# Running sums over four key tiles in an attention block, and values issued behind the scores

## The chip, the cores and the metric

The kernel runs on one core of one Trainium2 chip. Its time is the device time in microseconds, as the median of several runs. The engines are named as in the profile: PE (matrix products), PEld (its weight loads), DVE (vector), ACT (activations), POOL (GpSimd), SP (here only an issuer of DMAs). A name with a trailing q is an engine's sequencer, which issues DMAs and waits.

## The reference

One transformer block, on x of 2 x 1024 tokens x 1024 features, all in fp32:

```
h = layernorm(x)
q, k, v = split(h @ qkvw + qkvb)              # 32 heads of 32
x = x + softmax(q k^T / sqrt(32)) v @ ow + ob
h = layernorm(x)
x = x + (silu(h @ W_gate.T) * (h @ W_up.T)) @ W_down.T     # width 2752
```

The change is in the softmax and in the product with the values. For a head and a query, every exponential p[key] is needed twice: in the sum over keys of p[key] v[key], and in the plain sum over keys of p[key], by which the first is divided later.

## The kernel before

**Units and phases.** Attention is cut into 64 units. A unit is two heads (`u`), one half of a batch's queries (512), and all 1024 keys. Sixteen units make a phase: phase 0 is batch 0's first half of queries, phase 3 is batch 1's second half. A unit goes through its keys in NT = 8 tiles of 128 (`kt`). The probabilities of one key tile are a tile `p` of 128 keys x 1024 (512 queries of two heads); there is a ring of RING = 8 + 3 + 4 + 4 = 19 such buffers.

**What happens to a key tile.** `scores` (L500) makes two key tiles at a time: 8 PE instructions into two PSUM tiles `s`, at L509. DVE folds each into a running maximum `top` (`largest`, L525), and ACT copies it out into its `p` (`keep`, L528). When all eight are there, `maximum` (L541) reduces `top` over keys and spreads the negated maximum back over the partitions, through DRAM, as `m`. Then, tile by tile, `less_maximum` (L579) adds `m` (L582, on POOL, in phase 0 on DVE for every fourth tile), and `exponential` (L590) runs on ACT (L591). `values` (L610) multiplies with V: for each key tile four products of 256 columns (two heads, two halves of the queries), which use four column groups of PE at once. That is 8 PE instructions, at L620, into the PSUM tile `acc`.

**How the sums are made.** The plain sum over keys is also a PE product, with a matrix of `ones` in place of V (also at L620: again 8 PE instructions for a tile, called a block of ones here). To need fewer of these, tiles are first added in place: in phases 1 to 3 the odd tile gets the even one added (`add`, L601 to L605), and the ones product is made for odd tiles only (`summed`). In phase 0 the fourth tile of four also gets the second added, and the ones product is made once in four tiles. Since an in-place sum spoils the tile for the values, `differences` (L593, on POOL) rewrites V first: if p1 holds p0 + p1, then p0 (v0 - v1) + (p0 + p1) v1 is what was wanted. The adds run on DVE in phase 0, and on POOL and DVE by turns afterwards.

**Runs.** `values` is issued for RUN = 4 key tiles at a time, so each unit has two runs; in phases 1 to 3 a run is 16 instructions with V, a block of ones, and the same again. At the end of a unit ACT copies `acc` out (`finish`, L636), and SP stores the context and the sums (L644, L646). Once a quarter of a phase is done, POOL multiplies the context by the reciprocal sums (L730), for the output projection (L782).

**The order of the work.** Everything is in an order written out by the program. `attention_steps` (L650) writes a list of steps along score tiles n = 0, 1, 2, ...: each is a *beat*. At beat n it issues the scores (even n), the subtraction of the maximum for the tile NT + LAG = 11 beats back, and then the run of values that ended 14 beats back. `Emitter.run` (L66) interleaves this list with a list of filling work: the projections of q, k and v in phase 0, then the output projection and the feed-forward network of the phase before (its products are at L924 and L1073, and DVE adds the results at L1086). It keeps an estimated clock, on which each PE step costs its `cost` and everything else nothing. `em.later(delay, fn)` has a step issued when that clock is `delay` ns further on, and `needs=` holds a step back until what it names has been issued. None of this waits at run time: it only sets each engine's order of instructions, and each engine works through its own in that order.

Of the kernel before, what the change touches and what calls it, by code (L numbers as in the profile page):

```python
# [12 lines left out]
ALU = mybir.AluOpType  # L13
# [117 lines left out]
def preln_block_kernel(  # L131
# [14 lines left out]
    nc = tc.nc  # L146
# [3 lines left out]
    NT = S // P  # L150
# [9 lines left out]
    MM4, MM1 = 855.0, 230.0  # L160
    UNITS = HEADS // 2
    QTR = 4
    LAG = 3
    RUN = 4
    RING = NT + LAG + RUN + 4

    const = ctx.enter_context(tc.tile_pool(name="const", bufs=1))
    lin = ctx.enter_context(tc.tile_pool(name="lin", bufs=1))
# [25 lines left out]
    def Pt(name):  # L194
        return att.tile([P, S], F32, tag="p", bufs=RING, name=name)

# [32 lines left out]
    em = Emitter()  # L229
# [234 lines left out]
    class Unit:  # L464
# [35 lines left out]
        def scores(self, i):  # L500

            kts = (2 * i, 2 * i + 1)
            ps = [
                psum.tile([P, S], F32, tag="s", bufs=2, name=f"s_{self.name}_{kt}") for kt in kts
            ]
            for a in range(2):
                for h in range(2):
                    rows = slice((2 * a + h) * HD, (2 * a + h + 1) * HD)
                    nc.tensor.matmul(  # L509
                        ps[a][:, h * NH : (h + 1) * NH],  # L510
                        self.k[rows, i * P : (i + 1) * P],
                        self.q[rows, :],
                        start=True,
                        stop=True,
                    )


            for kt in kts:
                self.p[kt] = Pt(f"p_{self.name}_{kt}")

            def largest(kt, s):
                if kt == 1:
                    self.top = att.tile([P, S], F32, tag="top", bufs=1, name=f"top_{self.name}")
                if kt > 0:
                    nc.vector.tensor_tensor(self.top, s, self.p[0] if kt == 1 else self.top, ALU.max)  # L525

            def keep(kt, s):
                nc.scalar.copy(self.p[kt], s)  # L528

            if i == 0:  # L530
                keep(0, ps[0])
                em.later(2600.0, lambda: largest(1, ps[1]))
            else:
                largest(kts[0], ps[0])
                em.later(1600.0, lambda: keep(kts[0], ps[0]))
                em.later(1700.0, lambda: largest(kts[1], ps[1]))
            em.later(3300.0 if i > 0 else 4200.0, lambda: keep(kts[1], ps[1]))
            if kts[1] == NT - 1:
                self.maximum()
# [39 lines left out]
        def less_maximum(self, kt):  # L579
            p = self.p[kt]  # L580
            eng = nc.vector if self.phase == 0 and kt % 4 == 3 else nc.gpsimd
            eng.tensor_tensor(p, p, self.m, ALU.add)  # L582
            em.later(3500.0, lambda: self.exponential(kt))
            if kt % 2 == 1:
                twice = self.phase == 0 and kt % 4 == 3
                em.later(8100.0, lambda: self.add(kt, 1), None if twice else ("added", self.n, kt))
                if twice:
                    em.later(9900.0, lambda: self.add(kt, 2), ("added", self.n, kt))

        def exponential(self, kt):  # L590
            nc.scalar.activation(self.p[kt], self.p[kt], AF.Exp, scale=SCALE)  # L591

        def differences(self):  # L593

            v = self.v.rearrange("p (i a) n -> p i a n", a=2)
            nc.gpsimd.tensor_tensor(v[:, :, 0, :], v[:, :, 0, :], v[:, :, 1, :], ALU.subtract)
            if self.phase == 0:
                v = self.v.rearrange("p (i a) n -> p i a n", a=4)
                nc.gpsimd.tensor_tensor(v[:, :, 1, :], v[:, :, 1, :], v[:, :, 3, :], ALU.subtract)

        def add(self, kt, back):  # L601


            eng = nc.vector if self.phase == 0 or kt % RUN == RUN - 1 else nc.gpsimd
            eng.tensor_tensor(self.p[kt], self.p[kt], self.p[kt - back], ALU.add)  # L605

        def summed(self, kt):
            return kt % (4 if self.phase == 0 else 2) == (3 if self.phase == 0 else 1)

        def values(self, kt):  # L610

# [38 lines left out]
    def attention_steps(cuts):  # L650


        units = [Unit(n) for n in range(B * NS * UNITS)]
        lists = [Steps()]
        total = len(units) * NT
        q = lists[0]

        def load_step(k, i):
            if k < len(units):
                q.add(lambda: units[k].load(i), needs=("qk", units[k].b, units[k].g))  # L660

        for i in range(2):
            load_step(0, i)
        for n in range(total + NT + LAG + 3):
            if n in cuts:
                q = Steps()
                lists.append(q)
            k, kt = divmod(n, NT)
            if n < total:
                if kt == 1 or kt == 3:  # L670
                    load_step(k + 1, kt // 2)
                if n == 0:
                    q.add(lambda: em.later(9000.0, lambda: None, ("first",)))
                    q.add(lambda: None, needs=("first",))
                if kt == NT - 2:
                    q.add(units[k].load_v, needs=("v", units[k].b, units[k].hf))
            if n < total and kt % 2 == 0:
                q.add(lambda k=k, i=kt // 2: units[k].scores(i), MM4, beat=True)
            else:
                q.add(lambda: None, beat=True)  # L680
            k, kt = divmod(n - NT - LAG, NT)
            if 0 <= k < len(units):
                if kt == 0:
                    q.add(units[k].differences)
                q.add(lambda k=k, kt=kt: units[k].less_maximum(kt), needs=("max", k))
            k, kt = divmod(n - NT - LAG - 3, NT)
            if 0 <= k < len(units) and kt % RUN == RUN - 1:
                q.add(lambda: None, needs=("added", k, kt))
                for v in range(kt - RUN + 1, kt + 1):
                    cost = MM4 / 2 * (1 + units[k].summed(v))  # L690
                    q.add(lambda k=k, v=v: units[k].values(v), cost)
        return lists


# [453 lines left out]
    def weight_sum_steps():  # L1148
        q = Steps()

        def start(i):
# [42 lines left out]
            for j, args in enumerate(todo):  # L1194
                em.later(8500.0 + 3000.0 * j, lambda args=args: add(*args))
                em.later(16000.0 + 2500.0 * j, lambda j=j: store(j))
# [13 lines left out]
    with tc.manual_schedule():  # L1210
# [81 lines left out]

        rests = [rest(n) for n in range(B * NS)]
        lists = attention_steps([(n + 1) * UNITS * NT + 2 * NT for n in range(B * NS - 1)])
        side = [*prep_ctx(0), *prep_ctx(1)]
        em.run(head)
# [58 lines left out]
```

## Time and profile before

| | |
|---|---|
| runs before | 3269.68, 3277.49, 3278.75 us; median 3277.49 |
| profiled execution | 3264.24 us; span of its instructions 3262.5 us |
| granted TensorE clock, mean of the span | 0.996 |
| attention, first scores to last values | 90.8 to 2776.7 us |
| DVE adds L605, shortest / median / longest | 1162 / 1226 / 6904 ns |
| POOL adds L605, shortest / median / longest | 2342 / 2359 / 2827 ns |
| POOL busy in 200 us, 200 to 400 (phase 0) | 144.6 us |
| POOL busy in 200 us, 1200 to 1400 (phase 1) | 117.9 us |

In the lines of groups, "x480 | 1193.3, 2508 | 11.5 <-DVE top L525 8.4" reads: 480 instructions, 1193.3 us busy in all, 2508 ns each on average; the engine sat idle for 11.5 us in front of them, 8.4 of it until the DVE instruction at L525 was done. PE's instructions overlap each other, four at a time in the tiled products, so their duration is longer than the time from one start to the next. A fp32 product is two PE instructions. In a line of the timeline the first number is the start in us, the second the length, and a bracket at the end tells the idle time before it and what ended it.

### The profile page before, as it was taken

The numbers are of one execution on the slowest core, as the hardware profiler recorded it, in microseconds if no ns is written. First come the engines' busy times: TensorE is split into PE (matmuls) and PEld (weight loads), VectorE is DVE, ScalarE is ACT, GpSimd is POOL, SyncE is SP. The second block draws the span as 40 slices with busy tenths as digits, with TensorE's granted clock in tenths as the row PEclk, the third lists the DMA queues.
The fourth block names the chain that finished last, engine by engine and source line by source line (L and its number), as shares of the span: only waits on it lengthen the run. The fifth ranks groups of instructions, "written<-read, shape, count | busy, mean of one in ns | idle before, by whom it ended". The sixth has DMA issues, their size and how long they took to land.

```text
span 3262.5 us, 43853 instructions
## 1 busy us (share of the span) xinstructions
PE 3206.8 (98%) x16256; PEld 1792.5 (55%) x16256; DVE 1999.2 (61%) x2733; ACT 1432.7 (44%) x1570; POOL 1767.8 (54%) x871
## 2 busy tenths in 40 slices
PE   8999999999999999999999999999999999999999
PEld 4444444444346565663466555634666567477775
DVE  2266676666356677667766777676677774344334
ACT  2244554444456555554565555545655554010000
POOL 0267766776676555667766665667756555200000
PEclk9999999999999999999999999999999999999999
DMA  4566666655435444446344444463444444544442
GB/s 155 170 183 197 219 197 205 194 173 170 140 107 149 146 147 148 146 149 205 104 142 146 146 143 143 143 201 101 142 147 149 144 139 139 178 156 152 154 153 96
DMA packets 337828, 507.31 MB, mean 155 GB/s; under 512 B 105424, under 2 KB 122064, under 8 KB 337616
## 3 DMA queue, kind: packets, MB, share of 16 engines
q1 hardware_dynamic: 281424, 405.91, 39.9%
q10 hardware_dynamic: 56192, 98.60, 9.8%
q8 instruction: 130, 2.13, 0.3%
q14 instruction: 82, 0.67, 0.1%
HBM read 429.14 MB, written 75.24 MB: 155 GB/s over the span
## 4 chain that ended last, share of the span: by engine, by line
PE 86%; DVE 6%; DMA 3%; POOL 2%; issue 1%; ACT 1%; SPq 0%; ACTq 0%; POOLq 0%; DVEq 0%
PE p L924 31%; PE pq L370 11%; PE pd L1073 11%; PE acc L620 9%; PE s L509 7%; PE pvv L432 7%; PE po L782 7%; DVE top L525 1%; DVE x L1086 1%; POOL p L582 1%; DMA ctx<-dctx 1%; DMA rec<-drec 1%; PE pg L968 1%; PE pd L1000 1%; DVE p L605 1%
## 5 line engine op out<-in xcount | busy, mean ns | idle before, releaser
L582 POOL TENSOR_TENSOR p<-p,m 128x1024 f32<-128x1024 f32 x480 | 1193.3, 2508 | 11.5 <-DVE top L525 8.4
L528 ACT COPY p<-s 128x1024 f32<-128x1024 f32 x512 | 516.7, 1011 | 840.3 <-DVE top L525 642.1
L591 ACT ACTIVATE p<-p 128x1024 f32<-128x1024 f32 x512 | 533.2, 1057 | 270.0 <-POOL p L582 246.2
L525 DVE TENSOR_TENSOR top<-s,top 128x1024 f32<-128x1024 f32 x384 | 468.0, 1219 | 275.1 <-PE s L509 266.1
L924 PE MATMUL p<-sum,m 128*128 128x256 f32 x2688 | 616.7, 383 | 4.1 <-DVE sum L906 3.6
L924 PEld LDWEIGHTS p<-sum,m 128*128 128x128 f32 x2688 | 503.0, 190 | 126.5 <-issue 45.7
L605 POOL TENSOR_TENSOR p<-p,p 128x1024 f32<-128x1024 f32 x96 | 227.1, 2366 | 629.7 <-ACT p L591 595.6
L924 PE MATMUL p<-xn2T,m 128*128 128x256 f32 x2016 | 471.1, 383 | 5.2 <-DVE sum L833 2.4
L370 PE MATMUL pq<-xnT,wqk 128*128 128x512 f32 x1024 | 463.2, 601 | 0.0
L1073 PE MATMUL pd<-wp,h 128*128 128x512 f32 x960 | 438.0, 602 | 10.3 <-DVE x L1086 9.9
L924 PEld LDWEIGHTS p<-xn2T,m 128*128 128x128 f32 x2016 | 376.7, 190 | 104.4 <-issue 47.9
L605 DVE TENSOR_TENSOR p<-p,p 128x1024 f32<-128x1024 f32 x192 | 335.7, 1748 | 135.5 <-ACT p L591 134.8
L370 PEld LDWEIGHTS pq<-xnT,wqk 128*128 128x128 f32 x1024 | 188.2, 190 | 255.9 <-issue 252.7
L1073 PEld LDWEIGHTS pd<-wp,h 128*128 128x128 f32 x960 | 177.1, 190 | 248.1 <-issue 200.0
L509 PE MATMUL s<-q,k 32*128 32x512 f32 x2048 | 302.2, 643 | 10.6 <-ACT p L528 10.5
L1086 DVE TENSOR_TENSOR x<-pd,x 128x512 f32<-128x512 f32 x360 | 236.7, 681 | 71.1 <-PE pd L1073 70.6
L620 PE MATMUL acc<-p,vals 128*32 128x256 f32 x4096 | 266.2, 382 | 5.5 <-DVE p L605 5.4
L1186 POOL TENSOR_TENSOR ws<-raw 128x512 f32<-128x512 f32 x62 | 89.3, 1440 | 300.5 <-DMA raw<-in_w_gu 188.9
L432 PE MATMUL pvv<-wv,xnT 128*128 128x512 f32 x512 | 234.3, 603 | 2.4 <-ACT xnT L266 2.4
L782 PE MATMUL po<-wo,ctx 128*128 128x512 f32 x512 | 234.4, 608 | 0.0
L620 PEld LDWEIGHTS acc<-p,vals 128*32 128x32 f32 x4096 | 119.5, 109 | 147.3 <-issue 71.3
L952 ACT ACTIVATE gate<-gate 128x512 f32<-128x512 f32 x84 | 52.9, 630 | 278.0 <-DVE gate L951 277.4
(94 smaller groups left out, 2476.9 us busy)
## 6 DMA issues: line engine op xcount, KB each, us to landing
m<-dws SPq DMA_DIRECT2D x336, 256.0 KB
m<-in_w_gu SPq DMA_DIRECT2D x252, 256.0 KB
wp<-ddn SPq DMA_DIRECT2D x160, 256.0 KB
m<-d SPq DMA_DIRECT2D x64, 512.0 KB
wp<-in_w_dn SPq DMA_DIRECT2D x120, 256.0 KB
raw<-in_w_gu ACTq DMA_DIRECT2D x84, 256.0 KB
dws<-ws ACTq DMA_DIRECT2D x84, 256.0 KB
x<-in_x SPq DMA_DIRECT2D x32, 512.0 KB
```

Of the source, the lines that this page charges most:

```text
L370: nc.tensor.matmul(ps, wqk[b, g, w, hk][:, k, :], xnT[b, s][:, kc, :], start=(kc == 0), stop=(kc == KC - 1),)
L432: nc.tensor.matmul(st["ps"], xnT[b, t // TB][:, kc, (t % TB) * P : (t % TB + 1) * P], st["w"][kc], start=(kc == 0), stop=(kc == KC - 1),)
L509: nc.tensor.matmul(ps[a][:, h * NH : (h + 1) * NH], self.k[rows, i * P : (i + 1) * P], self.q[rows, :], start=True, stop=True,)
L525: nc.vector.tensor_tensor(self.top, s, self.p[0] if kt == 1 else self.top, ALU.max)
L528: nc.scalar.copy(self.p[kt], s)
L582: eng.tensor_tensor(p, p, self.m, ALU.add)
L591: nc.scalar.activation(self.p[kt], self.p[kt], AF.Exp, scale=SCALE)
L605: eng.tensor_tensor(self.p[kt], self.p[kt], self.p[kt - back], ALU.add)
L620: nc.tensor.matmul(self.acc[j * HD : (j + 1) * HD, c : c + NQ], w(h), self.p[kt][:, q0 : q0 + NQ], start=start, stop=stop, skip_group_chec ...
L782: nc.tensor.matmul(st["ps"], ctxT[b, blk][:, g, t * P : (t + 1) * P], st["w"][hf, g], start=(g == 0), stop=(g == G - 1),)
L924: nc.tensor.matmul(ps, mats[c, n][:, kc, :], rhs, start=(kc == 0), stop=(kc == hk - 1),)
L1073: nc.tensor.matmul(st["pd"], lefts[n](pi)[:, j, t * P : (t + 1) * P], st["wp", pi, n, j], start=(j == 0), stop=(j == PART // 2 - 1),)
```

## The change

There is now one scheme for all phases, SUMS = 4. In every run of four tiles the second gets the first added, the third the second, the fourth the third, so the fourth holds all four; the ones product is made for the fourth only. `differences` has three subtractions, v0 - v1, v1 - v2, v2 - v3, for all tiles of a unit at once. In phase 0 all adds are DVE's, issued 8.1 us behind the subtraction of the maximum; in the others the fourth tile's add is DVE's, 12.5 us behind, and the second and third tile's are POOL's, 11.0 us behind. An add whose predecessor has not been issued yet is put off by 0.5 us.

The run of values is issued one beat later, 15 beats behind its last tile, and directly behind that beat's scores, ahead of the subtraction of the maximum. A `p` buffer is taken when the score copy into it is issued, and no longer with the scores. The values of V are loaded one beat later too.

```diff
+    SUMS = 4
...
-            for kt in kts:
-                self.p[kt] = Pt(f"p_{self.name}_{kt}")
...
             def keep(kt, s):
+
+                self.p[kt] = Pt(f"p_{self.name}_{kt}")
                 nc.scalar.copy(self.p[kt], s)
...
             em.later(3500.0, lambda: self.exponential(kt))
-            if kt % 2 == 1:
-                twice = self.phase == 0 and kt % 4 == 3
-                em.later(8100.0, lambda: self.add(kt, 1), None if twice else ("added", self.n, kt))
-                if twice:
-                    em.later(9900.0, lambda: self.add(kt, 2), ("added", self.n, kt))
+            if kt % SUMS > 0:
+
+                vec = self.phase == 0 or kt % RUN == RUN - 1
+                delay = 8100.0 if self.phase == 0 else 12500.0 if vec else 11000.0
+                eng = nc.vector if vec else nc.gpsimd
+                em.later(delay, lambda: self.add(kt, eng))
...
-            v = self.v.rearrange("p (i a) n -> p i a n", a=2)
-            nc.gpsimd.tensor_tensor(v[:, :, 0, :], v[:, :, 0, :], v[:, :, 1, :], ALU.subtract)
-            if self.phase == 0:
-                v = self.v.rearrange("p (i a) n -> p i a n", a=4)
-                nc.gpsimd.tensor_tensor(v[:, :, 1, :], v[:, :, 1, :], v[:, :, 3, :], ALU.subtract)
-
-        def add(self, kt, back):
-
-
-            eng = nc.vector if self.phase == 0 or kt % RUN == RUN - 1 else nc.gpsimd
-            eng.tensor_tensor(self.p[kt], self.p[kt], self.p[kt - back], ALU.add)
+            v = self.v.rearrange("p (i a) n -> p i a n", a=SUMS)
+            for a in range(SUMS - 1):
+                nc.gpsimd.tensor_tensor(v[:, :, a, :], v[:, :, a, :], v[:, :, a + 1, :], ALU.subtract)
+
+        def add(self, kt, eng):
+
+            if kt % SUMS > 1 and ("added", self.n, kt - 1) not in em.done:
+                em.later(500.0, lambda: self.add(kt, eng))
+                return
+            eng.tensor_tensor(self.p[kt], self.p[kt], self.p[kt - 1], ALU.add)
+            em.done.add(("added", self.n, kt))
 
         def summed(self, kt):
-            return kt % (4 if self.phase == 0 else 2) == (3 if self.phase == 0 else 1)
+            return kt % SUMS == SUMS - 1
...
-        for n in range(total + NT + LAG + 3):
+        for n in range(total + NT + LAG + 4):
...
-                if kt == NT - 2:
+                if kt == NT - 1:
                     q.add(units[k].load_v, needs=("v", units[k].b, units[k].hf))
...
                 q.add(lambda: None, beat=True)
+
+            k, kt = divmod(n - NT - LAG - 4, NT)
+            if 0 <= k < len(units) and kt % RUN == RUN - 1:
+                q.add(lambda: None, needs=("added", k, kt))
+                for v in range(kt - RUN + 1, kt + 1):
+                    cost = MM4 / 2 * (1 + units[k].summed(v))
+                    q.add(lambda k=k, v=v: units[k].values(v), cost)
             k, kt = divmod(n - NT - LAG, NT)
...
-            k, kt = divmod(n - NT - LAG - 3, NT)
-            if 0 <= k < len(units) and kt % RUN == RUN - 1:
-                q.add(lambda: None, needs=("added", k, kt))
-                for v in range(kt - RUN + 1, kt + 1):
-                    cost = MM4 / 2 * (1 + units[k].summed(v))
-                    q.add(lambda k=k, v=v: units[k].values(v), cost)
```

## The prediction

> **What bounds the kernel now.** I read the page first, then the groups of instructions by shape, then the timeline of one stretch in the third phase of attention, then the waits, and last the start of the fourth phase. The page and the groups give the loads:
>
> ```profile
> span 3262.5 us, 43853 instructions
> PE 3206.8 (98%) x16256; PEld 1792.5 (55%) x16256; DVE 1999.2 (61%) x2733; ACT 1432.7 (44%) x1570; POOL 1767.8 (54%) x871
> ```
>
> ```profile
> L582 POOL TENSOR_TENSOR p<-p,m 128x1024 f32<-128x1024 f32 x480 | 1193.3, 2508 | 11.5 <-DVE top L525 8.4 <-DMA m<-d 3.0
> L605 DVE TENSOR_TENSOR p<-p,p 128x1024 f32<-128x1024 f32 x192 | 335.7, 1748 | 135.5 <-ACT p L591 134.8
> L605 POOL TENSOR_TENSOR p<-p,p 128x1024 f32<-128x1024 f32 x96 | 227.1, 2366 | 629.7 <-ACT p L591 595.6 <-DMA q<-dq 15.5 <-DMA m<-dws 9.7
> L620 PE MATMUL acc<-p,ones 128*32 128x256 f32 x1792 | 138.4, 381 | 0.0
> ```
>
> PE is busy 98% of the span; its idle time is 55.7 us in all, so the kernel's time is PE's work, and any PE instruction that goes away shortens it unless another engine then makes PE wait. The other engines have room on average: POOL 54%, DVE 61%. The timeline shows what a PE step really costs (matmuls overlap, so I read starts, not durations):
>
> ```profile
> 1704.72 5.31 PE L1073 MATMUL pd<-wp,h 128*128 128x512 f32 x12
> 1709.96 1.14 PE L509 MATMUL s<-q,k 32*128 32x512 f32 x8
> 1711.04 3.70 PE L1073 MATMUL pd<-wp,h 128*128 128x512 f32 x8
> 1714.67 1.07 PE L620 MATMUL acc<-p,vals 128*32 128x256 f32 x16
> 1715.55 0.61 PE L620 MATMUL acc<-p,ones 128*32 128x256 f32 x8
> 1715.99 1.05 PE L620 MATMUL acc<-p,vals 128*32 128x256 f32 x16
> 1716.85 0.61 PE L620 MATMUL acc<-p,ones 128*32 128x256 f32 x8
> 1717.39 1.98 PE L1073 MATMUL pd<-wp,h 128*128 128x512 f32 x4
> ```
>
> One block of ones (8 instructions) lasts from 1715.55 to 1715.99, 0.44 us. A run of values (four key tiles) stands alone between weight products, 3.6 us after the scores. Pairs of scores follow each other at about 10.2 us (1709.96, then 1720.17), so a score tile, the program's beat, is about 5.1 us.
>
> **The change on PE.** Phase 0 already summed over four tiles. Phases 1 to 3 summed over two, 48 units with four blocks of ones each; now two each. That takes away 48 x 2 = 96 blocks x 0.44 = 42.2 us of PE, with nothing put in its place on PE. (Before there are 1792 / 8 = 224 blocks; after, 128.) All of it lies on the path, since PE has no idle time to hide it in.
>
> Values also move behind scores. Each change between whole-array products and the tiled ones costs something: a 512-column instruction inside a stretch takes 0.43 us, so 12 of them from 1704.72 should end at 1709.88, and the scores start at 1709.96; the ones of 1716.85 should hand over at 1717.29 and do so at 1717.39. That is 0.08 to 0.10, say 0.09 us a change. Before, one run and its neighbouring scores have four such changes (into and out of each); after, three, if scores to values costs like the others. No scores stand directly before values in the trace, so the price of that change is open: free would save two changes, 0.18 x 128 runs = 23 us; twice as dear would save none, 0 us. The Trainium skill, TensorEngine Tiling (Array Packing), Key Properties, says that a change of tiling mode drains the engine, and scores (32 rows) and values (32 columns) are different modes, so I take the middle: 0.09 x 128 = 11.5 us. PE in sum: -53.7 us.
>
> **The sums on POOL and DVE.** The sum of a run is now a chain: tile 1 adds tile 0, tile 2 adds that, tile 3 adds that. In phases 1 to 3 tiles 1 and 2 are added on POOL, tile 3 on DVE; before, one add of each run was POOL's and one DVE's. So DVE keeps its 192 adds, POOL gets 96 more x 2.37 = 227 us. The differences of the values grow from one or two to three a unit. The small form (128x128) averages 630 ns against 880 for the old 128x256 one: 48 x (1.89 - 0.88) + 16 x 0.38 = 55 us. POOL goes from 1768 to about 2050 us. Per run of phases 1 to 3, about 20.4 us long, this is 2.9 us more. What covers it is POOL's own waiting (in the waits: total us, times, longest):
>
> ```profile
> POOL p L605 <- ACT p L591: 595.6, 80, 13.8
> ...
> DVE p L605 <- ACT p L591: 134.8, 48, 9.3
> ```
>
> and PE's own waits, which are few (total us, times, longest):
>
> ```profile
> PE s L509 <- ACT p L528: 10.5, 5, 3.9
> ...
> PE acc L620 <- DVE p L605: 5.4, 3, 2.1
> ```
>
> POOL runs ahead of the rest and then stands 7.4 us on average (595.6 / 80) before its one add of a run until ACT has made the exponential. An idle 7.4 us takes 2.9 more us of work without anybody noticing. The adds are also issued later: 11.0 us behind the subtraction on POOL and 12.5 us on DVE instead of 8.1, with the exponential still at 3.5, so POOL finds its operand ready more often. I cost the steady stretches at nothing on PE; if that cover were gone, ACT would wait for the late subtraction L582 in front of an exponential, its score copies behind it would be late, and PE would wait at L509.
>
> DVE now waits for POOL's second add. Behind that add in DVE's queue stand the evictions of the weight products (L1086 and its like) and the maxima, and PE waits for both. The POOL add of tile 2 is issued 12.5 + 5.1 - 11.0 = 6.6 us ahead of the DVE add and lasts 2.4, so POOL must be over 4.2 us behind before it hurts.
>
> A rule speaks against moving sums to POOL. The row: the DVE add with both inputs in SBUF averages 1748 ns, while the maximum of the same size that reads PSUM averages 1219. The Trainium skill, SBUF — State Buffer, Who interferes with whom, says that such a two-input DVE instruction and a POOL instruction reading SBUF exclude each other for the whole instruction. By the rule, POOL's share in phases 1 to 3 (1308 of 2042 us busy, by the view of stretches) rises by 275 / 2042 = 13 points, and of about 230 two-input DVE instructions there (96 adds, 63 of L954, some 70 of L1042 to L1048 and smaller ones) 30 more meet a POOL instruction; at the full 2.4 us each that is 72 us of DVE. By the row, the mean price of contention with POOL two thirds busy is 1748 - 1219 = 529 ns, so 13 points more of it make about 0.1 us x 230 = 24 us. DVE has some 35% idle in these phases, and only PE's waits for it count: L1086 costs PE 9.9 us in 360 instructions. Taken at the same proportion I put 2 us on PE; between -5 (later adds find the exponential done and hold DVE up less) and +10.
>
> **The starts of the phases.** Here the cover is gone. POOL multiplies the context and waits for its DMA, falls behind, and PE waits:
>
> ```profile
> 2150.01 1.27 POOL L730 TENSOR_TENSOR ctx<-ctx,rec 128x512 f32<-128x512 f32 x1 [9.25 <-DMA rec<-drec]
> ...
> 2162.54 1.26 POOL L730 TENSOR_TENSOR ctx<-ctx,rec 128x512 f32<-128x512 f32 x1 [2.89 <-DMA rec<-drec]
> ...
> 2235.16 2.35 POOL L605 TENSOR_TENSOR p<-p,p 128x1024 f32<-128x1024 f32 x1 [4.95 <-ACT p L591]
> ```
>
> ```profile
> 2160.14 2.99 PE L509 MATMUL s<-q,k 32*128 32x512 f32 x8 [3.57 <-ACT p L528]
> ```
>
> The scores at 2160.14 then take 2.92 us to the next start instead of 1.07: PE ran at half clock. From 2162.5 to 2235.2 POOL has almost no rest, 3.6 runs x 2.9 = 10 us more of backlog after the change. PE loses only what comes ahead of the peak of the lag: I take one added instruction, 2.4 us, and as much again for the slow clock, less what the DMA waits absorb: 4 us at each of three starts, 12 us. The ends are 0 (the added work fits in the DMA waits) and 40 (all 10 us, and 3.4 for the slow clock).
>
> **At nothing.** Score copies take their buffers when issued, and the second copy of a pair now writes over a tile that the values just behind the scores read; their first tile is done some 1.5 us (1.07 + 0.44) after the scores start, while the copies of the scores of 1709.96 start at 1713.80 and 1715.19. If PE were late there, ACT would stand. The load of the values moves one tile later on SP, together with the run that frees its buffer; POOL never idles for it at L596, and four tiles, 20 us, are left. The context's copy on ACT and its two stores on SP come one tile later with the values. At the end of attention 28.5 us of weight products cover the way to the output projection before, and I expect the same, since the program spreads them over the beats. In phase 0 DVE has the same three adds a run and more time.
>
> Sum: -42.2 - 11.5 + 2 + 12 = -39.7. The profiled execution took 3264.24 us (span 3262.5), so 3224.5 by its own measure; it stands 13.3 us under the median of the runs, 3277.49, from which I forecast 3238.
>
> **Rivals.** *PE takes all of it* (chance 0.25, us 3214 to 3228): the added POOL work disappears in DMA waits, the switch is cheaper, a few old stalls go. 3277.5 - 53.7 = 3224; with free switching 3212. For it: the 7.4 us of idle in every run. Against it: POOL's 72 us without rest.
> *The phase starts and contention eat it* (0.10, about 3274): +40 and +10 against -53.7. Changes within 0.3%, 10 us, are about what a measurement of this kernel can't tell from none.
> *DVE stands behind POOL's chain* (0.13, about 3337): the DVE add finishes 1 to 2 us ahead of the run now (1711.43 + 1.21 against 1714.67). One subtraction of 2.36 us in the way of the second POOL add in every run leaves 1.2 us uncovered: 96 x 1.2 = 113, less 53.7, is 59 us slower. It decides from 53.7 / 96 = 0.56 us a run. Against it: the 4.2 us of room and POOL's idle time.
> My own case has 0.52 and lies from 3229 to 3262. The range, 3214 to 3284, takes in the first rival but for its last few us, my case and the second; the third is left out. Faster: my case, the first, and the better end of the second, 0.78; same, the rest of the second, 0.08; slower, the third and a little beside it, 0.14.
>
> **What the profile will show.** Right: 1024 instructions acc<-p,ones instead of 1792; values that start directly behind scores; PE busy about 50 us less; POOL about 2050 us with its waits for ACT at L605 well below 595; DVE waits for POOL at L605 only after 895, 1500 and 2160. Wrong: PE idle far above 55.7 us, with L509 waiting for ACT or L1073 for DVE in the middle of phases, or a DVE wait for POOL in every run.

## The result, and the profile after

The changed kernel takes 3274.55 us (median), the kernel before 3269.38 in the same series: a ratio of 1.0020, 95% interval 1.0011 to 1.0029. It is 5 us slower where I forecast 40 us faster. The profiled execution has a span of 3277.5 us. Its page:

```profile
span 3277.5 us, 42696 instructions
PE 3163.8 (97%) x15488; PEld 1782.2 (54%) x15488; DVE 2072.7 (63%) x2733; ACT 1427.8 (44%) x1569; POOL 2066.3 (63%) x1079
...
L606 POOL TENSOR_TENSOR p<-p,p 128x1024 f32<-128x1024 f32 x192 | 469.4, 2445 | 334.2 <-ACT p L593 317.3
...
L606 DVE TENSOR_TENSOR p<-p,p 128x1024 f32<-128x1024 f32 x192 | 374.2, 1949 | 103.7 <-ACT p L593 61.9
```

PE did lose the work: 768 instructions fewer (15488 against 16256), 43 us less busy. Yet its idle time went from 55.7 to 113.7 us (span less busy), and POOL is at 2066 us, as forecast (2050). The same DVE adds now average 1949 ns, not 1748. PE's own waits name the new costs (total us, times, longest):

```profile
PE s L510 <- ACT p L529: 25.8, 9, 8.1
PE pd L1076 <- DVE x L1089: 25.1, 25, 2.5
PE acc L622 <- DVE p L606: 22.0, 10, 5.5
```

Before, these three were 10.5, 9.9 and 5.4. The view of the core adds the clock:

```profile
core 0: 3277.5 us, clock 0.987
```

Before it was 0.996. The records hold full and half speed only, so the time at half clock is twice the missing share: about 26 us before, 85 after. Half-clock stretches stand behind PE's waits, so PE loses part of such a wait a second time.

The new order on PE, from the timeline, is what the diff says, and prices the step that no trace had shown:

```profile
1907.47 1.14 PE L510 MATMUL s<-q,k 32*128 32x512 f32 x8
1908.55 1.56 PE L927 MATMUL p<-xn2T,m 128*128 128x256 f32 x6
1909.94 7.07 PE L927 MATMUL p<-sum,m 128*128 128x256 f32 x32
1916.85 0.59 PE L927 MATMUL p<-xn2T,m 128*128 128x256 f32 x2
1917.38 1.14 PE L510 MATMUL s<-q,k 32*128 32x512 f32 x8
1918.45 1.93 PE L622 MATMUL acc<-p,vals 128*32 128x256 f32 x32
1920.20 0.61 PE L622 MATMUL acc<-p,ones 128*32 128x256 f32 x8
1920.74 1.56 PE L927 MATMUL p<-xn2T,m 128*128 128x256 f32 x6
1922.14 5.31 PE L1076 MATMUL pd<-wp,h 128*128 128x512 f32 x12
```

From scores to values takes 1.07 us (1917.38 to 1918.45), from scores to weight products took 1.08 before (1709.96 to 1711.04). So at the hand-over the change of mode between scores and values costs what the others do, and one of four is saved, as forecast. There is one block of ones in the run.

The lines also show a price that the forecast left out. The 32 weight products from 1909.94 take 6.91 us to the next start, 0.216 each. The six right behind scores, from 1908.55, take 1.39, and the six right behind ones, from 1920.74, take 1.40: about 0.10 more than 6 x 0.216 = 1.30. So a return from tiled products to weight products costs 0.10 us inside the weight products too. Over the whole trace about 400 steps between weight products are longer by this before, and about 285 after. The new order has one return fewer in a run: 128 x 0.10 = 13 us saved on top of the 11.5, as an estimate.

Two pieces of the trace show where the time goes. The first is in the middle of a phase:

```profile
1938.87 2.81 POOL L583 TENSOR_TENSOR p<-p,m 128x1024 f32<-128x1024 f32 x1
...
1938.98 1.50 PE L622 MATMUL acc<-p,vals 128*32 128x256 f32 x24
1939.38 3.37 DVE L606 TENSOR_TENSOR p<-p,p 128x1024 f32<-128x1024 f32 x1
1941.64 3.35 POOL L606 TENSOR_TENSOR p<-p,p 128x1024 f32<-128x1024 f32 x1
...
1942.81 0.64 PE L622 MATMUL acc<-p,vals 128*32 128x256 f32 x8 [2.33 <-DVE p L606]
```

PE has done three tiles of a run and waits for the fourth, whose add is DVE's. That add comes after the run has begun, at 1939.38, during a POOL subtraction, and takes 3.37 us where 1.2 is its length undisturbed. The POOL add behind it takes 3.35 instead of 2.35.

The second is at the start of the fourth phase; POOL, ACT and PE in turn:

```profile
2176.35 1.27 POOL L733 TENSOR_TENSOR ctx<-ctx,rec 128x512 f32<-128x512 f32 x1 [7.82 <-DMA rec<-drec]
```

```profile
2183.92 1.06 ACT L593 ACTIVATE p<-p 128x1024 f32<-128x1024 f32 x1 [12.48 <-POOL p L583]
```

```profile
2189.70 2.99 PE L510 MATMUL s<-q,k 32*128 32x512 f32 x8 [8.06 <-ACT p L529]
```

POOL stands 7.8 us before the context's DMA, ACT 12.5 us before the subtraction that is queued behind it, PE 8.1 us before the score copies queued on ACT. The scores then run at half clock: the granted clock is 0.50 from 2183.7 to 2193.9.

### The profile page after: what moved, and what is told of

Same layout as the page of the kernel before. It is cut to its first block, busy times and chain, and to the rows that moved or that the text cites. A ratio compares the mean times of both kernels' runs of the same rounds, so it can differ in the third digit from the quotient of the medians.

```text
span 3277.5 us, 42696 instructions
## 1 busy us (share of the span) xinstructions
PE 3163.8 (97%) x15488; PEld 1782.2 (54%) x15488; DVE 2072.7 (63%) x2733; ACT 1427.8 (44%) x1569; POOL 2066.3 (63%) x1079
## 4 chain that ended last, share of the span: by engine, by line
PE 66%; DVE 8%; POOL 4%; DMA 3%; ACT 2%; issue 2%; ACTq 0%; SPq 0%; POOLq 0%; DVEq 0%
PE p L927 28%; PE pd L1076 10%; PE pq L371 6%; PE acc L622 6%; PE s L510 5%; PE po L785 5%; PE pvv L433 3%; POOL p L583 2%; DVE p L606 2%; DVE x L1089 1%; DVE top L524 1%; POOL p L606 1%; DMA k<-dk 1%; PE pg L971 1%; PE pd L1003 1%
## 5 line engine op out<-in xcount | busy, mean ns | idle before, releaser
L583 POOL TENSOR_TENSOR p<-p,m 128x1024 f32<-128x1024 f32 x480 | 1213.4, 2542 | 18.0 <-DMA m<-d 17.7
L606 POOL TENSOR_TENSOR p<-p,p 128x1024 f32<-128x1024 f32 x192 | 469.4, 2445 | 334.2 <-ACT p L593 317.3
L1076 PE MATMUL pd<-wp,h 128*128 128x512 f32 x960 | 436.8, 602 | 23.1 <-DVE x L1089 22.9
L371 PE MATMUL pq<-xnT,wqk 128*128 128x512 f32 x1024 | 456.4, 598 | 0.0
L606 DVE TENSOR_TENSOR p<-p,p 128x1024 f32<-128x1024 f32 x192 | 374.2, 1949 | 103.7 <-ACT p L593 61.9
L510 PE MATMUL s<-q,k 32*128 32x512 f32 x2048 | 308.6, 651 | 25.8 <-ACT p L529 25.8
L1076 PEld LDWEIGHTS pd<-wp,h 128*128 128x128 f32 x960 | 178.4, 190 | 261.1 <-issue 200.2
L1189 POOL TENSOR_TENSOR ws<-raw 128x512 f32<-128x512 f32 x62 | 96.5, 1557 | 302.7 <-DMA raw<-in_w_gu 205.7
L622 PE MATMUL acc<-p,vals 128*32 128x256 f32 x4096 | 256.3, 388 | 26.1 <-DVE p L606 22.0
```

The costliest lines, as they stand in the source:

```text
L371: nc.tensor.matmul(ps, wqk[b, g, w, hk][:, k, :], xnT[b, s][:, kc, :], start=(kc == 0), stop=(kc == KC - 1),)
L510: nc.tensor.matmul(ps[a][:, h * NH : (h + 1) * NH], self.k[rows, i * P : (i + 1) * P], self.q[rows, :], start=True, stop=True,)
L606: eng.tensor_tensor(self.p[kt], self.p[kt], self.p[kt - 1], ALU.add)
L622: nc.tensor.matmul(self.acc[j * HD : (j + 1) * HD, c : c + NQ], w(h), self.p[kt][:, q0 : q0 + NQ], start=start, stop=stop, skip_group_chec ...
L1076: nc.tensor.matmul(st["pd"], lefts[n](pi)[:, j, t * P : (t + 1) * P], st["wp", pi, n, j], start=(j == 0), stop=(j == PART // 2 - 1),)
```

## The experiments

Ratios are to the kernel before on the same chip, with their 95% intervals. The edits are to the changed kernel where nothing else is said.

**The two halves of the change alone.** First the order without the sums: the kernel before with

```diff
-            for kt in kts:
-                self.p[kt] = Pt(f"p_{self.name}_{kt}")
             def keep(kt, s):
+                self.p[kt] = Pt(f"p_{self.name}_{kt}")
...
-                if kt == NT - 2:
+                if kt == NT - 1:
                     q.add(units[k].load_v, needs=("v", units[k].b, units[k].hf))
...
                 q.add(lambda: None, beat=True)
+            k, kt = divmod(n - NT - LAG - 4, NT)
+            if 0 <= k < len(units) and kt % RUN == RUN - 1:
+                q.add(lambda: None, needs=("added", k, kt))
...
-            k, kt = divmod(n - NT - LAG - 3, NT)
-            if 0 <= k < len(units) and kt % RUN == RUN - 1:
-                q.add(lambda: None, needs=("added", k, kt))
...
```

> The kernel before with only the order changed: values one beat later and directly behind the scores, buffers taken at copying, V loaded one beat later; sums in twos in phases 1 to 3 as before (224 blocks of ones, POOL 96 adds). Theory A (POOL's added adds take the gain: they exclude DVE's two-input instructions and put POOL behind): this kernel has none of them, so it keeps the 0.09 x 128 = 11.5 us of the saved change of mode: about 3258 against before's 3269, PE idle near 56 us. Theory B (the new order itself makes PE wait, because values, scores and their copies now come in one burst and everything of POOL's is issued behind them): slower than before by 20 us or more, PE idle over 90 us.

3263.72 us, 0.9985 (0.9977 to 0.9994). A small gain, less than half of the 11.5 us. PE's work did fall, by 22.5 us of busy time (3206.8 before), about the 11.5 and the 13 from above:

```profile
PE 3184.3 (98%) x16256; PEld 1803.6 (55%) x16256; DVE 1948.3 (60%) x2733; ACT 1430.1 (44%) x1569; POOL 1762.0 (54%) x871
```

But PE's idle time rose from 55.7 to 71.9 us (span 3256.2): it stands twice, at 1520 and 2175, 22.8 us in all, before DVE's evictions, at the starts of phases. Theory B fell, but so did the idea that the order is free there. Then the sums without the order: `add`, `differences`, `summed` and their delays of the changed kernel, with values where they were.

> The kernel before with only the sums changed: four-tile chains, 96 more POOL adds, three differences a unit, adds issued 11.0 and 12.5 us behind; values stay where they were, three beats behind the last subtraction. Theory A: the 42 us of ones go and the stalls come, as in the changed kernel; without the 11.5 us of the order and with one beat less of room it is slower than the changed kernel: about 3285 to 3300, PE idle over 110 us. Theory B: without the new order the gain of 42 us shows: about 3230.

3362.99 us, 1.0296 (1.0281 to 1.0311): far worse than any theory had it. The wait is one that I had not reckoned with at this size:

```profile
PE acc L622 <- DVE p L606: 109.9, 64, 5.6
```

The fourth tile's add, issued 12.5 us behind the subtraction, comes too late for values three beats behind. So the later values are what makes the late adds bearable at all.

**POOL's second add.** Left out in phases 1 to 3, then kept but cut out of DVE's chain (both kernels leave a part of the sum out):

```diff
+            if self.phase == 0 or kt % SUMS != 2:
                 eng.tensor_tensor(self.p[kt], self.p[kt], self.p[kt - 1], ALU.add)
```

```diff
+            back = 2 if self.phase > 0 and kt % SUMS == 3 else 1
-            eng.tensor_tensor(self.p[kt], self.p[kt], self.p[kt - 1], ALU.add)
+            eng.tensor_tensor(self.p[kt], self.p[kt], self.p[kt - back], ALU.add)
```

> The changed kernel without POOL's second add of a run in phases 1 to 3 (the third tile's; its sum is left out of the ones product, so the output is not the reference's). PE's work is the same as in the changed kernel. Theory A: all of the lost gain comes back, PE idle falls from 114 to about 56 us and the time to 3269 - 54 = 3215. Theory B: it stays within 15 us of the changed kernel, 3260 to 3275. A third theory, C (the three differences of V on POOL cost it, not the adds): little comes back either.

> The changed kernel with the same instructions on every engine, but DVE's add of the fourth tile in phases 1 to 3 reads the second tile and not the third, so DVE doesn't wait for POOL's second add (one term of the sum is left out). Theory A1 (the harm is the new wait of DVE for POOL's chain, with the evictions queued behind it): about 3230, the DVE waits for POOL at the add, 42 us, gone. Theory A2 (the harm is POOL's load and the exclusion of the two engines): within 10 us of the changed kernel's 3275.

Without the add 3259.03 us, 0.9974 (0.9965 to 0.9983): 15 us came back, at the edge of theory B and far from theory A's 3215. With the chain cut 3284.62, 1.0051 (1.0036 to 1.0065): nothing came back, though DVE's wait for POOL's add fell from 41.7 to 5.7 us. So this wait, which I had priced in the forecast, is not what costs. Why the cut kernel is 10 us slower than the uncut one stays open; DVE's add is then free to start while POOL is at its second one.

**Reading or occupying.** To tell POOL's time from its reading, the second add became three fills of the same tile, 0.95, 0.96 and 0.31 us on average (the tile's product with V is then wrong too):

```diff
+            if self.phase > 0 and kt % SUMS == 2:
+                nc.gpsimd.memset(self.p[kt], 0.5)
+                nc.gpsimd.memset(self.p[kt], 0.5)
+                nc.gpsimd.memset(self.p[kt][:, : S // 4], 0.5)
+            else:
+                back = 2 if self.phase > 0 and kt % SUMS == 3 else 1
+                eng.tensor_tensor(self.p[kt], self.p[kt], self.p[kt - back], ALU.add)
```

> The changed kernel with POOL's second add of a run in phases 1 to 3 replaced by fills of the same tile that only write, about 2.4 us in all; DVE's last add reads the second tile (so that tile's values and sum are left out). It occupies POOL as long as in the run with the chain cut (3285 us), but reads nothing. Theory X (DVE's instructions with two inputs in SBUF are held up by POOL instructions that read): DVE's adds come back to about 1750 ns from 1949, and the time to that of the run without the add, about 3260. Theory Y (POOL's occupied time is what costs, whatever it does): 3275 to 3285.

3252.52 us, 0.9961 (0.9946 to 0.9975), 32 us under the cut chain. The cut chain's page and this one's:

```profile
PE 3164.7 (97%) x15488; PEld 1782.8 (54%) x15488; DVE 2059.9 (63%) x2733; ACT 1426.7 (44%) x1569; POOL 2066.2 (63%) x1079
...
PE 3156.3 (97%) x15488; PEld 1782.4 (55%) x15488; DVE 2015.0 (62%) x2733; ACT 1427.1 (44%) x1569; POOL 2046.4 (63%) x1271
```

POOL is nearly as busy, DVE 45 us less, and the time is no longer than without the add (0.9961 against 0.9974). Theory X holds: POOL's occupied time costs nothing measurable, an add that also reads does. Part of the 32 us may be the cut chain's own unexplained 10; against the changed kernel it is 22. That the fills are shorter pieces than an add was not tested apart. The Trainium skill, SBUF — State Buffer, Who interferes with whom, says just this: a DVE instruction with two SBUF inputs contends with a POOL instruction that reads SBUF, not with one that only writes. DVE's adds moved little (1877 to 1826 ns, where theory X had 1750), but h<-gate,up, also of two SBUF inputs and on the way to PE's next product, fell from 1331 to 1071 ns, against 692 ns undisturbed.

**The third tile's add on DVE** in phases 1 to 3, to spare POOL:

```diff
-                vec = self.phase == 0 or kt % RUN == RUN - 1
-                delay = 8100.0 if self.phase == 0 else 12500.0 if vec else 11000.0
+                vec = self.phase == 0 or kt % RUN > 1
+                delay = 8100.0 if self.phase == 0 else 12500.0 if kt % RUN == RUN - 1 else 11000.0
```

> The changed kernel with the third tile's add in phases 1 to 3 on DVE and not on POOL (POOL 96 adds as before, DVE 288). Theory A (POOL's load): PE waits fall as in the run without this add, 3259 to 3265. Theory E (DVE is what PE waits for in the middle of phases, at the evictions and at the last add): DVE gets 96 x about 1.75 = 168 us more, 63% to 68%, PE waits longer at L1089 and L606: about 3290.

3315.5 us, 1.0141 (1.0123 to 1.0160). POOL was relieved by 179 us, DVE got 134 more, and PE waits longer for evictions (54.8 us at two lines, 25.1 before this edit). That is theory E's direction, 25 us beyond its number: it is DVE that PE waits for, at the evictions, though not at the last add (22.0 to 9.3 us). DVE also stands longer before POOL's add (75.3 us against 41.7), so its load and this wait are not separated here.

**When the adds are issued.** The delays of phases 1 to 3, changed one at a time and together, as POOL / DVE in us (changed kernel 11.0 / 12.5):

```diff
-                delay = 8100.0 if self.phase == 0 else 12500.0 if vec else 11000.0
+                delay = 8100.0 if self.phase == 0 else 10500.0 if vec else 8100.0
```

> The changed kernel with the adds of phases 1 to 3 issued 8.1 us (POOL) and 10.5 us (DVE) behind the subtraction instead of 11.0 and 12.5. Theory F (the adds come too late for the values: the 22 us that PE waits at L622 for the DVE add): these 22 us go and the time falls to about 3250. Theory G (adds stand in front of unfinished exponentials when issued earlier, and hold POOL's subtractions and DVE's evictions up): slower than 3275, by 5 to 20 us.

> The changed kernel with only POOL's adds issued earlier (8.1 us behind the subtraction instead of 11.0), DVE's left at 12.5. Theory F1 (the DVE add is late because it waits for POOL's chain, which is issued late): nearly all of the 22 us that both together brought, about 3255. Theory F2 (DVE's own place in its queue is late): at most 5 us, about 3270.

> The changed kernel with only DVE's adds of phases 1 to 3 issued earlier (10.5 instead of 12.5 us behind), POOL's left at 11.0. Theory F2: most of the 22 us, about 3256. Theory F1: DVE comes to its add sooner but POOL's is no sooner done, so DVE stands there with the evictions behind it: 3275 or slower, with the waits of DVE for POOL's add over the 42 us of the changed kernel.

> The changed kernel with the adds of phases 1 to 3 issued 6.5 us (POOL) and 8.5 us (DVE) behind the subtraction; early adds were 8.1 and 10.5. Theory S: room for all runs is already there at 10.5 (2 of 96 late), so nothing more: 3250 to 3258. Theory P: a different place among POOL's instructions, a different share of exclusion; DVE's adds away from 1574 ns by over 150 either way, and the time with them by 10 us. Theory G (adds in front of unfinished exponentials): POOL's wait for ACT grows from 354 us and the time by 5 to 15 us.

| POOL / DVE | us | ratio (95%) |
|---|---|---|
| 11.0 / 12.5 (the change) | 3274.55 | 1.0020 (1.0011 to 1.0029) |
| 8.1 / 12.5 | 3277.93 | 1.0031 (1.0020 to 1.0041) |
| 11.0 / 10.5 | 3250.27 | 0.9953 (0.9936 to 0.9970) |
| 8.1 / 10.5 | 3252.11 | 0.9945 (0.9929 to 0.9961) |
| 6.5 / 8.5 | 3277.51 | 1.0024 (1.0014 to 1.0034) |

In the first four rows only DVE's delay matters, and 2 us of it are worth 24 us. Theory F2. With 11.0 / 10.5 PE's wait at the values falls from 22.0 to 6.8 us and DVE's adds from 1949 to 1700 ns, so the add has both more room and a better place among POOL's instructions. With DVE's adds two us earlier still, and POOL's 1.6, all is lost again, by another wait: DVE stands before ACT's exponentials (100.2 us, 66.6 at 8.1 / 10.5), and gates and evictions behind it are late (these lines had 17.1, 4.7 and nothing at 8.1 / 10.5):

```profile
PE pd L1076 <- DVE x L1089: 22.3, 29, 3.4
PE p L927 <- ACT gate L939: 15.8, 11, 3.8
PE pd L1003 <- DVE x L1014: 13.4, 2, 6.9
```

There is no line here for the DVE add at L606: theory S holds for the late side, theory G for the early side, with a loss of 25 us where it had 5 to 15. The same early adds with values at their old place:

> Only the sums changed, values at their old place (three beats behind the last subtraction), with the early adds (8.1 and 10.5 us). Sums at the old place with late adds took 3363 us, the DVE add ended on the median 2.1 us after its run had started. Theory S (what counts is the room between the DVE add and its run): 2 us earlier brings the median to about 0, so PE still waits in many runs: 3280 to 3310. Theory P (what counts is where the add falls among POOL's instructions): the DVE add falls where it does in the run with early adds, about 3255 to 3265 plus the 5 us of the order.

3288.96 us, 1.0061 (1.0048 to 1.0073): PE's wait for the DVE add is 54.7 us, half of the 109.9 above, but there. Theory S: the beat of delay for the values is needed for the sums too. It is worth 37 us here (3289 against 3252), but 22.6 of these are PE's own work (3184.8 against 3162.2 us busy), which the new order saves anyway, and 13 are idle time.

With early adds, POOL's second add was left out again:

> The early adds (8.1 and 10.5 us) without POOL's second add in phases 1 to 3 (its term is left out of the sum). What is left of the loss against 3269 - 54 = 3215 when both late adds and added POOL work are gone. If the two are separate costs, 22 + 15 us: about 3237. If the late adds cost only because POOL's chain is longer: no more than the early adds alone, about 3250.

3219.77 us, 0.9855 (0.9835 to 0.9875). Now the add is worth 32 us, where it was worth 15 behind late adds. Without it PE's wait for the evictions of the weight products falls from 17.1 to 9.5 us, at the scores from 28.7 to 22.0. The two losses hide each other in part.

**The starts of the phases.** POOL multiplies the context 5 us behind the issue of its loads; issued later, it should no longer block its queue:

```diff
-            em.later(5000.0, go, ("mult", b, blk, i))
-            em.later(8000.0, lambda: None, ("prep", b, blk, i))
+            em.later(14000.0, go, ("mult", b, blk, i))
+            em.later(17000.0, lambda: None, ("prep", b, blk, i))
```

> The changed kernel with POOL's multiplication of the context by the reciprocal sums issued 9 us later (14.0 instead of 5.0 us behind its loads), so that POOL no longer stands in front of a DMA that has not landed with all its subtractions queued behind. Theory D (a large part of the loss is at the starts of phases: POOL stands before the context's DMA, ACT's exponentials, DVE's add and the evictions stand behind POOL, and PE loses 8 to 12 us in one piece and then runs at half clock): PE's long waits at 888, 1520 and 2190 go, 25 to 35 us with the slow clock: about 3243. Theory A (steady load and exclusion of POOL and DVE): under 10 us, about 3267.

> Only the new order (sums in twos), with the context's multiplication 9 us later. Theory D: the two waits of 12 us at 1520 and 2175 go, with the half clock behind them, 25 to 30 us: about 3237 against 3264 without. Theory A says nothing here; without D it stays at 3264.

3290.71 us, 1.0060 (1.0039 to 1.0080), and 3285.73, 1.0049 (1.0034 to 1.0064). Both miss theory D's number, and the first shows why: the wait at the scores is cured (25.8 to 7.4 us), a new one takes its place.

```profile
PE po L785 <- POOL ctx L733: 39.6, 4, 18.1
```

The output projection can't spare 9 us. So a smaller dose, 8.0 and 11.0 us, in four kernels:

> Early adds, and the context's multiplication on POOL issued 3 us later (8.0 instead of 5.0 us behind its loads; 9 us later let PE wait 40 us for the context). Theory D at a small dose: the long waits at 1516 and 2172 (6 and 10 us) shrink by 3 us each and no wait for the context appears: about 3244. If any delay shows at the projection: 3252 to 3260.

> The kernel before with the context's multiplication issued 3 us later (8.0 instead of 5.0). With early adds the 3 us brought 34 us. If that was paid by the change (values one beat later, POOL fuller), before has little of it: its waits at the starts are 4.5, 1.8 and 4.2 us with 14 us of half clock, so 8 to 15 us at most: about 3258. If the starts of before suffer as much: about 3240.

> The changed kernel, late adds left, with the context's multiplication issued 3 us later. If late adds and starts of phases are separate costs: 3274 - 34 = 3240. If they hide each other: 3255 or more.

> Early adds, later context and no second add on POOL in phases 1 to 3 (its term is left out of the sum). With the starts of phases relieved, this tells what the added POOL work costs in the steady stretches. If POOL's added work cost its 32 us at the starts: 3212 to 3218, hardly below the 3218 with it. If it costs in the steady stretches (exclusion of DVE): 3190 to 3200.

| context 3 us later, in | us | ratio (95%) | same without |
|---|---|---|---|
| the kernel before | 3249.14 | 0.9940 (0.9927 to 0.9952) | 1 |
| the changed kernel | 3242.93 | 0.9924 (0.9912 to 0.9937) | 1.0020 |
| with early adds (8.1 / 10.5) | 3218.06 | 0.9845 (0.9832 to 0.9857) | 0.9945 |
| and no second POOL add | 3188.82 | 0.9760 (0.9747 to 0.9774) | 0.9855 |

The second row is where separate costs would put it (3240), the fourth next to the forecast for a cost in the steady stretches. The third came 26 us under its forecast: 3 us brought 34, not 8. The first lies between its theories.

The third row leaves no part of the work out and is faster than both kernels, by 51.7 us against the one before. Its view of the core, and what is left of PE's waits for ACT:

```profile
core 0: 3217.1 us, clock 0.994
```

```profile
PE s L510 <- ACT p L529: 10.2, 12, 1.9
```

No single wait at the scores is longer than 1.9 us now. The old kernel gains as well, 19 us, from the same three us: in its profiled execution PE's wait at the scores falls from 10.5 to 3.7 us, and the clock rises from 0.996 to 0.998.

## Why the prediction was wrong, point by point

The last table reads as a ledger, since its rows differ by one step each. Against the kernel before with the same context delay, the changed one is 3249 - 3243 = 6 us faster (their intervals overlap); early adds bring 25 more, no second add 29 more, 60 in all. Of the pages of its first and last rows:

```profile
PE 3199.8 (98%) x16256; PEld 1790.3 (55%) x16256; DVE 1998.2 (62%) x2733; ACT 1431.7 (44%) x1570; POOL 1769.4 (54%) x871
...
PE 3133.6 (98%) x15488; PEld 1776.7 (56%) x15488; DVE 1970.2 (62%) x2733; ACT 1428.1 (45%) x1569; POOL 1794.5 (56%) x983
```

- **PE's saved work: right in kind, too small.** I forecast 42.2 + 11.5 = 53.7. PE is busy for 66 us less in the last row than in the first (3199.8 to 3133.6). The order's term is the small one: I priced the hand-over and missed the 0.10 us inside the weight products behind it. Of the 66 the time shows 60, since PE's idle time went from 49.0 to 54.3 us. This last row still has the three differences on POOL, which leaves theory C little.
- **"I cost the steady stretches at nothing on PE": wrong, by 29 us,** and this is the step that failed first. I covered 2.9 us of POOL work a run by POOL's 7.4 us of idle time. POOL did have the time: with fills in place of adds it was nearly as busy and nothing was lost. What the added work takes is DVE's access, not POOL's time. The forecast did weigh this, at 24 us of DVE by its row and 72 by the rule. Measured, the second add costs DVE 49 us behind late adds (2072.7 against 2024.0 us busy) and 28 behind early ones (2001.1 against 1973.3), between the two. The error came after: I let 2 us of it, at most 10, reach PE, because DVE is idle 35% of the time. But PE waits for DVE at evictions and gates, three PSUM buffers deep. That a single instruction of 1.2 us that takes 3.4 is late there whatever the average, is argued from stretches like the one at 1939 and was not counted.
- **"Later adds find the exponential done and hold DVE up less": wrong sign, 25 us.** This is the second step that failed. DVE did wait less for ACT (134.8 to 61.9 us), as forecast. I did not ask who waits for the add. The lines were there: in the timeline of before the add ended 2.0 us before its run began (1712.64 against 1714.67), and the change moved the add by 4.4 us for one beat of about 5, which at best keeps so small a margin. I used it in the third rival alone, and blamed POOL's chain for eating it. That mechanism is refuted: the cut chain gave nothing back. The place in DVE's own queue was enough. Whether the add's room or its better place among POOL's instructions gives more of the 25 us was not separated; the runs with values at the old place show that room counts.
- **The starts of the phases: 12 us forecast.** The context's delay gives 31 to 32 us to the changed kernel (1.0020 to 0.9924) and 19 to the old one, so the change's own part is about 12. That this is the forecast's number is in part luck: the delay takes away only what 3 us can, and with early adds it brought 34. The old kernel's part I had not seen as a cost that can be taken away. Of the 2.92 us that scores take behind a long wait, I put all down to the half clock; twice 1.07 is 2.14, and the rest stays open.
- **In sum:** -60 + 29 + 25 + 12 = +6, measured +5. This closes because each term is a difference of two rows; it is no test. The forecast had -53.7 + 2 + 12. The rows were measured in one order, and the second add was worth only 15 us behind late adds, so the split between 29 and 25 holds for this order. Their sum holds without the context's delay as well: there both together gave 3274.55 - 3219.77 = 55 us.
- **What would be seen.** Fewer ones, values behind scores, POOL at 2050 us and its waits for ACT below 595 came as listed. DVE's waits for POOL are five, 41.7 us, at the starts of phases, as listed. The sign for wrong that I named, PE idle far above 55.7 us with L1076 waiting for DVE in mid-phase, is the one that came.
- **The rivals.** The second, contention and phase starts eating the gain, had the time right (3274) and 0.10 of the chance. That is luck: it meant 4 us faster than a median of 3277.49, from three runs, and twenty runs gave 3269.38. Its ends were 10 for contention and 40 for the starts; the ledger has 29 and 12, and 25 more that it did not have.

## What to carry to other kernels

Idle time of an engine covers added work only if that work takes nothing from the engine that the bound one waits for; ask what the added instruction shares with that engine. Where an instruction is moved later in a queue because its operands come later, look up the margin to its consumer first: here 2 us in the issue time of one add were worth 24 us, and 2 us earlier still, with POOL's adds moved too, lost them again. And when a change that saves measured work brings nothing, look for the waits that took it before giving it up: other delays for the adds and for the context made the same change 52 us faster than the start. (19 of these the old kernel gains too, from the context's delay alone.)

## What the runs showed of the hardware

POOL fills that only write did not disturb DVE as a POOL add of about the same length did: DVE was busy for 45 us less and this kernel 32 us faster. At the hand-over, a change of PE from row tiles to column tiles costs what one from row tiles to whole-array products does (1.07 against 1.08 us from the start of the scores to the next product). Weight products behind tiled ones lose about 0.10 us more, inside their own stretch. A PE wait of 8 us was followed by a granted clock of 0.50 until 2193.9: the waits at the starts of phases cost their own length and part of it again.
